# A masked maximum per head in one VectorE instruction, with the planner's slots regrouped

## The chip, the cores and the metric

One core of a Trainium2 chip runs the whole program. The metric is the device time of one execution in microseconds, from inputs in DRAM to the output in DRAM. Three runs of the kernel before took 1297.30, 1300.51 and 1302.75 us; the median is 1300.51 us.

## The reference, cut to what matters

The input is 16 sequences (batches) of 256 tokens with 256 features, in float32. Each batch goes through one block in hyperbolic space (a norm with scale and shift from a condition, full attention with 16 heads of 16 features, Möbius addition, a feed-forward part), then through a second attention with a local and a remote part, a modulated linear layer, and a feed-forward layer with four low-rank experts of which two are chosen. The change is about the scores of the second attention. Its local part lets a token see the 64 tokens that end with itself:

```python
i = jnp.arange(W)[:, None]
j = jnp.arange(2 * W)[None, :]
base = (j > i) & (j <= i + W)
...
sc = jnp.einsum('bhnid,bhnjd->bhnij', Qb, Kw) / np.sqrt(D).astype(np.float32)
sc = jnp.where(mask[None, None], sc, -jnp.inf)
p = jax.nn.softmax(sc, axis=-1)
```

The softmax subtracts, for each token and head, the greatest score among the tokens that the mask lets through. That maximum is what the changed lines compute.

## The kernel before, in words

**The batches.** `front(b)` records the first block of batch b, `back(b)` the second attention and the experts. All 16 batches are recorded, one after the other; nothing runs at that point.

**The planner.** `Plan` keeps one node per instruction (several products of TensorE that belong together are one node, a `unit`). At the end `emit` (L214) orders them. `schedule` (L254) simulates the five queues: PE (TensorE), DVE (VectorE), ACT (ScalarE), POOL (GpSimd) and SP, which issues the DMAs. `cost` (L182) gives each operation a time, `lag` the delay until another engine may use its result. Each node has a due time: its batch's number times a period, less the longest chain behind it. Of the nodes that can start first on their engine, the one due first is taken. `emit` tries 32 settings (hurry, period, limit of narrow banks), keeps the one whose simulated end is earliest, and writes the queues out in that order. Work of several batches is thus interleaved in every queue, and the order is fixed before the program starts.

**Memory.** PSUM has eight banks of 512 float32 columns. A product takes a bank when it starts and the bank is free after its last reader; `four` takes four banks for one stage. In SBUF, `spare` tiles come from three common pools: 6 slots of 1 KB per partition (t1), 18 of 2 KB (t2) and 8 of 4 KB (t4). `w_tile` gives a tile a ring of its own: pqk and qk2 with one slot of 8 KB each, p1o and p2o with one of 2 KB, xr with two of 2 KB, and xpT, gkm and gkT with one small slot each. A ring's next tile waits for all users of the one that had its slot. Small statistics (`s_tile`, L624) have rings of two, x has a ring of four.

**The local maximum.** For each batch there are four stages: two groups of features c, and two blocks of 128 query tokens qt. The first block sees 128 key tokens, the second 192. A stage fills four banks, one per quarter j of the 128 rows; in a bank lie the scores of two heads side by side, 256 or 384 columns. First four products of `ident_bf` and `maskq` (bfloat16, 128 rows deep) write the mask into the banks: 0 where a token is seen, -1e30 elsewhere (L1046). Then four score products, 32 rows deep and run beside each other in the array, add to them (L1048). Last, VectorE reduces each bank to two maxima with one `tensor_reduce` (L1054). The remote part has a stage of its own in the same manner, with `maskrq` (L1062, L1065, L1071). The 24 maxima of a token are transposed (L1077), go through DRAM (mT_dram, L1079) and come back as a row of the query tiles (L1083), so that the later score products (L1103 remote, L1166 local) give scores with the maximum taken off.

**Other lines that the prediction uses.** L784 is `project`, a product of a transposed tile with weights. L840 is the first projection to q, k and v, L974 the projection to the second q and k, L1211 the modulated linear layer, L939 the feed-forward part in the first block. L699 is the transposing of a tile through TensorE. L733 is the scale and shift behind the norm. L745 is a product of two tiles on VectorE whose sum goes to an accumulator. L872 scales q, k and v of the heads, L920 divides the first attention's result by its sum. L1289 and L1298 are the experts' low-rank and wide products; the low-rank rows come back through DRAM (low_dram). L372 is `load`, which issues the DMAs of weights.

Of the kernel before, what the change touches and what calls it, by code (L numbers as in the profile page):

```python
# [44 lines left out]
N_T1, N_T2, N_T4 = 6, 18, 8  # L45
# [20 lines left out]
class Plan:  # L66
# [5 lines left out]
    PERIODS = 65.0, 70.0, 75.0, 80.0  # L72
    HURRIES = 5.0, 6.0, 7.0, 8.0
    early = ("pqk", "qk2")
    NARROWS = 3, 4

    def __init__(self, tc):
        nc = tc.nc
        self.tc, self.nodes, self.batch, self.hold = tc, [], 0, None
        self.seen, self.slots, self.ring, self.kept, self.wide = {}, {}, {}, set(), set()  # L80
        self.phys, self.place = {}, {}
        self.real = {"pe": nc.tensor, "dve": nc.vector, "act": nc.scalar, "pool": nc.gpsimd, "sp": nc.sync}
# [46 lines left out]
    def region(self, ap, write=False):  # L129
        name, dims = ap.name if isinstance(ap, View) else ap.tensor.name, list(ap.ap)  # L130
        if ap.space == DRAM and write:
            return name, 0, P, ap.offset, ap.offset + 1
        if ap.space in (PSUM, DRAM):
            return name, 0, P, 0, 1 << 30
        step = dims[0][0]
        p0, f0 = divmod(ap.offset, step)
        return name, p0, p0 + dims[0][1], f0, f0 + 1 + sum((n - 1) * st for st, n in dims[1:])

    def note(self, eng, op, args, kw):
# [7 lines left out]
        first = self.region(outs[0])[0]  # L147
# [4 lines left out]
        if not joins:  # L152
            n = dict(
                eng=eng, ops=[], cost=0.0, batch=self.batch, pre=set(), post=set(), tiles=set(),
                id=len(self.nodes), hold=self.hold, first=first, table=None, modes=[],
# [4 lines left out]
        n["cost"] += self.cost(eng, op, outs, rest, n)  # L160
        for write, aps in ((False, rest), (True, outs)):
            for ap in aps:
                if is_ap(ap):
                    self.access(n, write, *self.region(ap, write))
# [17 lines left out]
    def cost(eng, op, outs, rest, n):  # L182

        cols = max(int(np.prod(v.shape[1:])) for v in outs + [r for r in rest if hasattr(r, "tensor")])
        if eng == "sp":
            run = min((v.ap[-1][1] if v.ap[-1][0] == 1 else 1 for v in outs + rest if hasattr(v, "tensor")), default=1)
            return 0.1 + int(np.prod(outs[0].shape)) * 4 / (2e5 if run >= 128 else 0.7e5 if run >= 32 else 0.05e5)
        if eng == "pe":
# [8 lines left out]
            if n["hold"] is not None and (lhs.shape[0] < 64 or outs[0].shape[0] < 64):  # L197
                return (0.024 if lhs.shape[0] < 64 else 0.016) + 0.00042 * cols
# [7 lines left out]
        if eng == "pool":  # L206
            if op == "affine_select":
                return 0.2 + 0.00098 * cols
            return 0.76 if ALU.pow in rest else 0.27 + (0.0021 if op == "tensor_tensor" else 0.0009) * cols
        extra = 0.06 * (op == "scalar_tensor_tensor") + 0.05 * (op == "tensor_reduce") + 0.06 * (len(outs) > 1)  # L210
        return max(0.11, 0.05 + 0.0011 * cols + extra)


    def emit(self):  # L214
# [5 lines left out]
        for tag, names in self.ring.items():  # L220
            bufs = self.slots[names[0]][1]
            for old, new in zip(names, names[bufs:]):
                behind = [m["id"] for m in users[old]]
                for u in users[new]:
                    if tag in self.early and u["eng"] != "pe":
                        for m in [nodes[m] for m in u["pre"]]:
                            if m["eng"] == "pe" and m["batch"] == u["batch"]:
                                m["pre"].update(behind)
# [5 lines left out]
        lag = lambda n: {"pe": 0.27, "sp": 2.2, "dve": 0.18, "act": 0.18}.get(n["eng"], 0.05)  # L234
# [10 lines left out]
        settings = itertools.product(self.HURRIES, self.PERIODS, self.NARROWS)  # L245
        best = min(settings, key=lambda s: self.schedule(order, users, lag, *s)[0])
        _, out, self.place = self.schedule(order, users, lag, *best)
# [6 lines left out]
    def schedule(self, order, users, lag, hurry, period, most):  # L254
# [16 lines left out]
        held, narrow = set(), 0  # L271
# [4 lines left out]
        table, mode, out = None, None, []  # L276

        def start(n):
# [5 lines left out]
            for tag, names in need.items():  # L284
                if len(pools[tag]) < len(names):
                    return None, need
                if tag == "bank" and names[0] not in self.wide and narrow + len(names) > most:
# [4 lines left out]
        while len(out) < len(nodes):  # L292
            best = None
            for e, ns in avail.items():
                cand = [(max(t, free[e]), n, need) for n in ns for t, need in [start(n)] if t is not None]
# [26 lines left out]
            n["t"], n["end"] = t, end  # L322
            out.append(n)
# [1041 lines left out]
```

## Time and profile before

| | us |
|---|---|
| median of three runs | 1300.51 |
| profiled execution, device time | 1302.17 |
| its span, first to last instruction | 1300.4 |
| PE busy (share of the span) | 1207.1 (93%) |
| DVE busy | 877.3 (67%) |
| ACT busy | 688.2 (53%) |
| POOL busy | 666.2 (51%) |
| mask products L1046, busy, 256 of them | 46.5 |
| local score products L1048, busy, 512 records | 52.5 |
| local maxima L1054, busy, 256 of them | 119.9 |

The profile comes from one execution. A float32 product leaves two records in it, a bfloat16 product one. PE is TensorE's products and PEld its weight loads. Busy time of PE is the union of modelled spans, so a product's time in the queue is better read from one start to the next. In a row of the groups, the idle time stands behind the second bar with what ended it. The granted clock of TensorE was 0.972 of full speed on the mean.

### The profile page before, as it was taken

What the parts mean: (1) busy time and instruction counts of PE and PEld (TensorE: products, weight loads), DVE (VectorE), ACT (ScalarE), POOL (GpSimd) and SP (SyncE); (2) the same over time, 40 slices, a digit from 0 to 9 for tenths busy, and PEclk for the clock granted to TensorE, in tenths of its full rate; (3) what the DMA queues carried; (4) which work ended last, traced back from release to release, by engine and by line L of the source; (5) the groups of instructions that cost most, each with busy time, mean ns of one, the idle gap of its engine ahead of it and who ended that gap; (6) DMA issues with size and microseconds to landing.
All of it is one profiled execution on the core that took longest, in us unless ns stands there. A gap on an engine that the chain in (4) does not pass through costs nothing.

```text
span 1300.4 us, 27101 instructions
## 1 busy us (share of the span) xinstructions
PE 1207.1 (93%) x9684; PEld 797.8 (61%) x9684; DVE 877.3 (67%) x2800; ACT 688.2 (53%) x1750; POOL 666.2 (51%) x1677
## 2 busy tenths in 40 slices
PE   4987999999999999999999999999999998979776
PEld 2654565757666576657666576657656665757465
DVE  5747686876869677776869677676968765573331
ACT  1555667547473755647473755646473753724210
POOL 5167566646464564646464564656455462743210
PEclk7998999999999999999999999899999999999897
DMA  6520001010100201010100101020000100000001
GB/s 193 175 61 17 23 7 35 25 29 10 40 14 18 36 17 30 16 36 9 41 14 18 35 18 31 7 43 11 23 23 17 25 2 20 1 15 7 20 2 25
DMA packets 59462, 38.70 MB, mean 30 GB/s; under 512 B 33312, under 2 KB 53792, under 8 KB 59328
## 3 DMA queue, kind: packets, MB, share of 16 engines
q1 hardware_dynamic: 59328, 36.97, 11.6%
q8 instruction: 76, 1.25, 0.5%
q14 instruction: 58, 0.48, 0.1%
HBM read 31.60 MB, written 5.36 MB: 28 GB/s over the span
## 4 chain that ended last, share of the span: by engine, by line
PE 65%; DVE 11%; POOL 10%; ACT 6%; DMA 4%; issue 3%; SPq 0%; DVEq 0%; ACTq 0%; POOLq 0%
PE bank L784 11%; PE bank L1298 6%; PE bank L904 5%; PE bank L840 5%; PE bank L891 4%; PE bank L699 4%; PE bank L939 4%; PE bank L1048 3%; PE bank L1289 2%; PE bank L1211 2%; PE bank L1153 2%; POOL t L566 2%; PE bank L1046 2%; PE bank L974 2%; ACT t L662 2%
## 5 line engine op out<-in xcount | busy, mean ns | idle before, releaser
L566 POOL TENSOR_SCALAR_AFFINE_SELECT t<-t 128x512 f32<-128x512 f32 (+2 forms) x264 | 168.2, 661 | 37.7 <-ACT t L1174 36.8
L662 ACT ACTIVATE t<-t 128x256 f32<-128x256 f32 x224 | 92.8, 423 | 148.0 <-DVE t L733 53.4
L911 ACT ACTIVATE t<-bank 128x512 f32<-128x512 f32 x256 | 132.3, 615 | 38.8 <-PE bank L904 38.6
L784 PE MATMUL bank<-wot,t 128*128 128x256 f32 x512 | 129.2, 394 | 2.1 <-POOL t L1311 1.9
L1054 DVE TENSOR_REDUCE maxima<-bank 128x2 f32<-128x384 f32 (+1 forms) x256 | 119.9, 482 | 15.1 <-PE bank L1048 15.0
L1298 PE MATMUL bank<-t,wi 128*128 128x256 f32 x512 | 130.0, 389 | 0.0
L784 PEld LDWEIGHTS bank<-wot,t 128*128 128x128 f32 x512 | 93.2, 192 | 28.0 <-issue 11.8
L1174 ACT ACTIVATE t<-bank 128x320 f32<-128x320 f32 x256 | 92.9, 446 | 19.8 <-PE bank L1166 19.3
L1298 PEld LDWEIGHTS bank<-t,wi 128*128 128x128 f32 x512 | 91.5, 192 | 18.2 <-issue 9.0
L840 PE MATMUL bank<-wqkv,t 128*128 128x512 f32 (+1 forms) x256 | 94.8, 504 | 1.4 <-ACT t L708 1.4
L699 PE MATMUL bank<-ident,t 128*128 128x128 f32 x384 | 61.4, 284 | 18.0 <-DVE t L733 11.7
L904 PE MATMUL bank<-t,t 32*128 32x512 f32 x512 | 75.7, 646 | 0.1
L1311 POOL TENSOR_TENSOR t<-t,t 128x512 f32<-128x512 f32 x32 | 43.3, 1368 | 53.4 <-DVE t L1308 52.3
L891 PE MATMUL bank<-t,vpad 128*32 128x256 f32 x1024 | 68.3, 385 | 0.1
L699 PEld LDWEIGHTS bank<-ident,t 128*128 128x128 f32 x384 | 43.8, 142 | 39.2 <-DVE t L733 13.8
L844 DVE SCALAR_TENSOR_TENSOR pqk<-bank,m1f,bqkv 128x512 f32<-128x512 f32 (+1 forms) x64 | 38.9, 614 | 40.6 <-PE bank L840 31.2
L840 PEld LDWEIGHTS bank<-wqkv,t 128*128 128x128 f32 x256 | 45.7, 193 | 33.0 <-issue 25.2
L1166 PE MATMUL bank<-qk 32*128 32x128 f32 (+1 forms) x1024 | 58.9, 330 | 6.8 <-ACT t L1174 4.8
L1304 ACT ACTIVATE t<-bank 128x512 f32<-128x512 f32 x64 | 36.3, 593 | 53.1 <-PE bank L1298 53.1
L708 ACT COPY t<-bank 128x512 f32<-128x512 f32 x80 | 47.5, 593 | 31.6 <-PE bank L699 31.4
L1308 DVE SCALAR_TENSOR_TENSOR t<-bank,t 128x512 f32<-128x512 f32 x64 | 42.3, 681 | 29.9 <-PE bank L1289 29.7
L1166 PEld LDWEIGHTS bank<-qk 32*128 32x128 f32 x1024 | 45.4, 189 | 27.3 <-issue 12.3
(322 smaller groups left out, 2856.1 us busy)
## 6 DMA issues: line engine op xcount, KB each, us to landing
ada<-ada_dram SPq DMA_DIRECT2D x32, 256.0 KB
x<-in_x_dram SPq DMA_DIRECT2D x16, 256.0 KB
ada<-ada_dram SPq DMA_DIRECT2D x32, 128.0 KB
out_dram<-t SPq DMA_DIRECT2D x16, 256.0 KB
qk<-in_w_f_dram SPq DMA_DIRECT2D x2, 1024.0 KB
t<-low_dram SPq DMA_DIRECT2D x64, 32.0 KB
t<-rho_dram SPq DMA_DIRECT2D x16, 128.0 KB
t<-in_w_ada_dram SPq DMA_DIRECT2D x3, 512.0 KB
```

What stands on the lines that cost most here:

```text
L566: pool.affine_select(out=ap, in_=ap, pattern=pattern, compare_op=ALU.is_ge, fill=fill, base=base, channel_multiplier=cm,)
L662: act.activation(junk, src, AF.Square, accum_out=dst)
L699: pe.transpose(ps[:, c, bass.ts(t, P)], src[:, t, bass.ts(c, P)], ident)
L784: pe.matmul(ps[:, t, :], chunks[c][:, bass.ts(t, P)], weights[:, c, :], start=c == 0, stop=c == n - 1)
L840: pe.matmul(ps[:, :w], uT[:, c, bass.ts(t, P)], wqkv[:, c, a : a + w], start=c == 0, stop=c == NC - 1,)
L891: pe.matmul(avs[c][quad(j), gh, :], vpad[:, kt, head(2 * c + gh, j), :], es[j][:, gh, :], start=kt == 0 and gh == 0, stop=kt == NT - 1, sk ...
L904: pe.matmul(scs[j], kT[quad(j), c, bass.ts(kt, P)], qT[quad(j), c].rearrange("p g s -> p (g s)"), start=True, stop=True,)
L911: act.activation(es[j].rearrange("p g s -> p (g s)"), scs[j], AF.Exp)
L1054: dve.tensor_reduce(mx[:, qt, m0 : m0 + 4 * NC + 1 : 4 * NC], scs[j][:, : 2 * w].rearrange("p (g w) -> p g w", g=2), AX.X, ALU.max,)
L1166: pe.matmul(scs[j][:, a : a + w], k2T[quad(j), g % 2, g // 2, bass.ts(kt, P)], q2T[quad(j), g % 2, g // 2, kt * P : kt * P + w], start=Tru ...
L1174: act.activation(e[:, k, 0:NLOC], scs[2 * pr + k][:, :NLOC], AF.Exp)
L1298: pe.matmul(hs[j][:, f, :], wi[:, c, bass.ts(2 * j + f, P)], zT[:, c, :], start=False, stop=c == NC - 1, skip_group_check=True,)
```

## The change: what it does

The four mask products of each local stage are left out. In place of one reduction per bank there are two `tensor_tensor_reduce` instructions, one for each head: each adds the mask (float32, in SBUF) to the scores in the bank, writes the sums to a bfloat16 tile `seen` that nobody reads, and puts the greatest into its column of `mx`. The remote stage keeps its mask products.

```diff
                 with plan.unit():
-                    for j in range(4):
-                        pe.matmul(scs[j][:, : 2 * w], ident_bf, maskq[:, 2 * a : 2 * (a + w)], start=True, stop=False)
                     for j in range(4):
                         pe.matmul(
                             scs[j][:, : 2 * w], qm[quad(j), c, bass.ts(qt, P)], km[quad(j), c, :, k0 : k0 + w],
-                            start=False, stop=True,
+                            start=True, stop=True,
                         )
                 for j in range(4):
-                    m0 = 4 * c + j
-                    dve.tensor_reduce(
-                        mx[:, qt, m0 : m0 + 4 * NC + 1 : 4 * NC],
-                        scs[j][:, : 2 * w].rearrange("p (g w) -> p g w", g=2), AX.X, ALU.max,
-                    )
+                    for gh in range(2):
+                        m = 4 * (NC * gh + c) + j
+                        dve.tensor_tensor_reduce(
+                            out=seen[:, :w], in0=scs[j][:, gh * w : (gh + 1) * w], in1=maskf[:, a : a + w], scale=1.0,
+                            scalar=NEG, op0=ALU.add, op1=ALU.max, accum_out=mx[:, qt, m : m + 1],
+                        )
```

The slots are regrouped. The rings of `w_tile` are gone, and their tiles come from the common pools: pqk as two tiles pq (one per token block), qk2 as q2T and k2T. The preamble's large tiles (biases, w_f1, w_f2) take common slots too and are loaded in more pieces.

```diff
-N_T1, N_T2, N_T4 = 6, 18, 8
+N_X = 6
+N_T1, N_T2, N_T4 = 6, 20, 11
...
-    PERIODS = 65.0, 70.0, 75.0, 80.0
-    HURRIES = 5.0, 6.0, 7.0, 8.0
-    early = ("pqk", "qk2")
-    NARROWS = 3, 4
+    SETTINGS = ((7, 80, 5, 1), (8, 75, 5, 1), (6, 70, 5, 0), (10, 75, 4, 1), (3, 45, 3, 0))
...
     def s_tile(shape, tag, b):
-        return plan.tile(stat, [P] + shape, tag, f"{tag}_{b}", 2, True)
+        bufs = 6 if tag in ("m1n2", "m1f", "m2n2", "m2f", "w1") else 4 if int(np.prod(shape)) <= 32 else 3
+        return plan.tile(stat, [P] + shape, tag, f"{tag}_{b}", bufs, True)
```

The planner changes with them. A product may claim, in its own node, the SBUF tiles that its result goes to, so that it isn't started before they are free (`claim`). It can be made to wait for a tile that a later instruction of its chain reads or overwrites (`wait_for`, `wait_free`). Regions of a tile are kept apart more finely (`regions`). Costs and lags have new numbers, a fifth setting holds back batches that aren't the oldest, and a DMA has a time of issue on SP and a time of transfer behind it, with at most eight under way:

```diff
+        if eng == "pe":
+            n["tiles"].update(self.claims)
+            self.claims = []
...
-            run = min((v.ap[-1][1] if v.ap[-1][0] == 1 else 1 for v in outs + rest if hasattr(v, "tensor")), default=1)
-            return 0.1 + int(np.prod(outs[0].shape)) * 4 / (2e5 if run >= 128 else 0.7e5 if run >= 32 else 0.05e5)
+            long = all(v.ap[-1][0] == 1 and v.ap[-1][1] >= P for v in outs + rest)
+            n["move"] = int(np.prod(outs[0].shape)) * 4 / (2.2e5 if long else 1.1e5)
+            return 0.4 if long else 0.7
...
+                since = free[e] if e != "sp" or len(landed) < 8 else max(free[e], landed[-8])
...
+            if e == "sp":
+                end = moved = max(end, moved) + n["move"]
+                landed.append(end + lag(n))
```

Some instructions are split by token block, so that a tile of each block can be used by itself: the scaling of q, k and v (L872) and the division of the remote heads (L1126, L1127), for instance

```diff
         for k, (eng, dst) in enumerate(((dve, qn), (dve, kn), (dve, vpad))):
-            eng.tensor_tensor(
-                dst[:, :, :, 0:HD], pq[:, :, k],
-                fh.rearrange("p (t k) h -> p t k h", k=3)[:, :, k].unsqueeze(3).to_broadcast([P, NT, H, HD]),
-                ALU.mult,
-            )
+            for t in range(NT):
+                eng.tensor_tensor(
+                    dst[:, t, :, 0:HD], pq[t][:, k],
+                    fh.rearrange("p (t k) h -> p t k h", k=3)[:, t, k].unsqueeze(2).to_broadcast([P, H, HD]),
+                    ALU.mult,
+                )
```

and the eight transposes that bring an attention's result of one token block back to tokens are one unit (`to_tokens`). What is computed stays the same.

## The prediction

> **What bounds the kernel now.** I read the busy shares first, then the slices, then three stretches, then the groups of the engines involved.
>
> ```profile
> PE 1207.1 (93%) x9684; PEld 797.8 (61%) x9684; DVE 877.3 (67%) x2800; ACT 688.2 (53%) x1750; POOL 666.2 (51%) x1677
> ...
> PE   4987999999999999999999999999999998979776
> ...
> PEclk7998999999999999999999999899999999999897
> ```
>
> TensorE is the engine near its limit, but not everywhere: the first four slices and the last five have holes. The stretches put numbers on that (length, then busy time of PE, PEld, DVE, ACT, POOL, the granted clock).
>
> ```profile
> 0.00:130.00 130.00, 97.58 (x528) 59.46 (x528) 82.69 (x289) 59.44 (x146) 65.82 (x183) 0.89 0.38 112
> 130.00:1100.00 970.00, 943.13 (x7796) 615.68 (x7794) 710.95 (x2261) 564.20 (x1443) 535.84 (x1365) 0.99 0.10 23
> 1100.00:1300.40 200.40, 166.42 (x1366) 122.67 (x1362) 83.68 (x251) 64.55 (x163) 64.50 (x129) 0.91 0.06 12
> ```
>
> TensorE is idle for 32.4 us at the start, 26.9 us in the 970 us of the middle (2.8%), and 34.0 us at the end. In the middle VectorE is busy 73% of the time, so TensorE sets the pace there, and a product taken out of its queue should be time taken off the end.
>
> [...] The timeline decides, since it shows starts and not modelled ends:
>
> ```profile
> 323.09 0.81 PE L1046 MATMUL bank<-maskq,ident_bf 128*128 128x384 bf16 x4
> 323.83 0.93 PE L1048 MATMUL bank<-t,t 32*128 32x384 f32 x8
> 324.58 1.04 PE L1289 MATMUL bank<-t,wb 32*128 32x256 f32 x16
> ...
> 339.29 0.60 PE L1046 MATMUL bank<-maskq,ident_bf 128*128 128x256 bf16 x4
> 339.82 0.71 PE L1048 MATMUL bank<-t,t 32*128 32x256 f32 x8
> 340.46 1.13 PE L1211 MATMUL bank<-t,cw 128*128 128x256 f32 x4
> ```
>
> Each group starts before the busy time of the one in front is over, and no idle time stands at any of these rows: the queue is full, and the distance from start to start is the real price.
>
> **Part 1: the mask products go.** There are 256 of them (16 batches, 4 stages, 4 banks), half 256 and half 384 columns wide. Four narrow ones take 339.82 - 339.29 = 0.53 us, four wide ones 323.83 - 323.09 = 0.74 us. The difference, 0.21 us for 4 x 128 columns, is 0.053 us per 128 columns, so the columns of four narrow ones take 0.43 us and of four wide ones 0.64 us; about 0.10 us is left in both cases. I read that as the change from 128 rows to 32 rows of the array, and it stays, since the 32-row score products still follow something 128 rows wide. So a stage loses 0.43 or 0.64 us: 32 x (0.43 + 0.64) = **34.2 us**. Upper bound: all of 32 x (0.53 + 0.74) = 40.6 us, if that 0.10 goes too. Lower bound: only the stages in the full stretch count, 970 of 1300 us, 25.5 us, because at the ends TensorE waits for others.
>
> **Part 2: VectorE's maximum.** 256 reductions, each over two heads of one bank, become 512 fused instructions of one head each (128 or 192 elements), each with an accumulator read. The nearest rows (behind the first bar the busy time in us and the mean ns of one, behind the second the idle time in front):
>
> ```profile
> L1054 DVE TENSOR_REDUCE maxima<-bank 128x2 f32<-128x384 f32 x128 | 67.8, 547 | 9.9 <-PE bank L1048 9.9
> L1054 DVE TENSOR_REDUCE maxima<-bank 128x2 f32<-128x256 f32 x128 | 52.1, 417 | 5.2 <-PE bank L1048 5.1
> ...
> L745 DVE SCALAR_TENSOR_TENSOR t<-p1o,t 128x256 f32<-128x256 f32 x32 | 12.8, 420 | 0.1
> ...
> L745 DVE DVE_READ_ACCUMULATOR t<-p1o,t 128x1 f32 x32 | 2.6, 81 | 0.0
> ```
>
> From 256 to 384 elements a reduction grows by 130 ns. L745 is the nearest to the new one: two streams and an accumulator, 420 ns for 256 elements, hence 290 ns for 128 and 355 ns for 192. By whole durations with the read behind them the pair costs 2 x (290 + 81) - 417 = 325 ns more than the narrow reduction, and 2 x (355 + 81) - 547 = 325 ns more than the wide one: 83 us over 256 pairs. That is the upper bound, since in the timeline durations on VectorE overlap: from start to start a narrow reduction takes 0.33 us and a wide one 0.46 us, L745 takes 0.346 us, and the instruction after an accumulator read starts together with it. On that scale the new ones are 0.346 - 0.13 = 0.21 and 0.28 us, and a pair costs 0.09 us more: 24 us over the run. I take 24 us, being what the queue really pays. It lies beside TensorE: VectorE in the middle goes from 73% of a batch's 73 us to some 77% of 71 us (82% by the upper bound). Without that cover it would cost 1.5 us a batch. How long four banks are held hardly changes: 0.43 to 0.64 us less in front, 4 x 0.09 = 0.37 us more behind. A cost below nothing is excluded: more instructions read the same elements.
>
> [...]
>
> **Part 3: VectorE work split per token block.** Normalised q, k and v (L872) become 96 instructions of 256 elements for 48 of 512; at 701 ns against 414 ns (L920, the same shape from a bank) that is 0.13 x 48 = 6 us. The reciprocal and product of the remote heads are halved too: 16 x (0.25 + 0.15) = 6 us. Both beside TensorE: 0.8 us a batch more. Bounds: nothing and 12 us of VectorE.
>
> **Part 4: loads and slots at the start.** Weights and bias for the preamble come in six more DMAs; an issue of L372 shows 0.42 to 0.44 us on the DMA queue of SP, so 2.6 us there. TensorE waits for a load only once (5.4 us, the first w_ada). Nothing to 2.6 us; I take nothing, because work of batch 0 covers the rest.
>
> **Part 5: the planner.** Its costs, limits and buffer rules change, and it writes out the order of every queue anew. SP's transfers are no longer summed on SP but given a landing time and a limit of eight; a product now claims, when it starts, the SBUF tile that its result goes to. What it can gain is what TensorE waits for now:
>
> ```profile
> PE bank L1103 <- DMA t<-mT_dram: 17.6, 3, 7.5
> PE bank L699 <- DVE t L733: 11.7, 3, 10.4
> PE bank L1289 <- DMA t<-low_dram: 10.7, 1, 10.7
> ```
>
> These three, 40 us, fall almost wholly at the two ends, where few batches are there to fill a gap; a better order moves them little. In the middle 27 us are spread over many short waits. Bounds: -60 us (all of the middle, half of the 66 us at the ends) and +80 us (5 us a batch, the slower rival below). I take half of the middle: **-13 us**, the ends unchanged. That is nearest to what the waits show, and it is the softest term here.
>
> **Sum**, against the profiled execution: its time 1302.2 us is the span of 1300.4 and 1.8 around it, 0.1% over the median of 1300.5. 1302.2 - 34.2 - 13 = 1255 us, with the added VectorE work hidden. What is late next in the middle is still TensorE.
>
> **Rivals.**
>
> 1. *The order gains much more.* The three long waits shrink as landing times are modelled, and deeper common buffers fill the start. For it: 66 us of idle at the ends. Against: the last batch's chain through two round trips to DRAM stays. -34 and -40 to -60: some 1222 us.
> 2. *The gain is eaten.* VectorE at 82% in bursts holds the four banks of a stage longer, and the products behind wait; the new order gains nothing. For it: 15 us of VectorE's waits at L1054 show that it works at the pace of TensorE. Against: it has a quarter of its time free. 0.325 - 0.09 us x 64 stages x 1 to 2 banks uncovered returns 15 to 30 us: 1302 - 34 + 22 = 1290 us, a range of 1283 to 1298.
> 3. *Slower: slots run out.* The rings of their own (pqk, qk2, p1o, p2o, xr and three small ones) are gone. Counted in kilobytes per partition, the 4 KB class with pqk and qk2 had room for 12 tiles and has 11; with p1o, p2o and two of xr the 2 KB class had 22 and has 20. Per batch some 16 tiles ask for the 4 KB class, and q2T and k2T are held from the projection at L974 to the last local scores. A product that claims its target waits in TensorE's queue with everything behind it. It decides when such waits exceed the gain: (34 + 13) / 16 = 2.9 us a batch over what is waited now. At 5 us a batch: 1302 - 34 + 80 - 13 = 1335 us. Against: the common pool is given by need, and the planner counts the slots when it orders.
> 4. *It does not do what it says*: the products gone but the 0.10 us change of array shape doubled. That is at most 64 x 0.10 = 6 us, inside the forecast's range.
>
> **How the numbers follow.** Forecast 1255 us (1238 to 1275), chance 0.55; rival 1, 0.20; rival 2, 0.14; rival 3, 0.11. Rival 2's upper edge is partly within 0.5% of 1300.5 us (about what a measurement of this kernel can tell from no change), so 0.05 of its chance goes there. Faster 0.84, same 0.05, slower 0.11. The range leaves out rival 3 and the far half of rival 1: 1218 to 1290 us.
>
> **What would show it.** Right: no bf16 products against the mask in TensorE's groups apart from the remote ones (L1062, L1099), busy time of PE down by 30 to 45 us, the score products at the same distance from start to start, 512 fused instructions with mean durations near 290 and 355 ns, VectorE's busy time up by 20 to 95 us, and a batch in the middle at 70 to 71 us. Wrong: fused instructions above 500 ns, idle time of PE in the middle above 60 us with waits on banks at L1048 or on tiles at L974, or a start and an end longer than 130 and 200 us.

## The result and the profile after

The changed kernel takes **1363.53 us** (median of four runs, 1359.61 to 1366.12), the kernel before 1301.45 us beside it: a ratio of **1.048 [1.0445, 1.0516]**. It is slower; the forecast was 1255 us. The profiled execution took 1366.12 us, its span is 1364.4 us.

The page of the changed kernel, with the rows that answer to those of before, and the first line of the chain that ended last:

```profile
PE 1229.7 (90%) x9418; PEld 820.1 (60%) x9428; DVE 932.0 (68%) x3646; ACT 678.6 (50%) x1742; POOL 652.1 (48%) x1677
...
PE   5999888988989998998999899998999998899776
...
PEclk8999878988999899999999998999999899899797
...
PE 48%; DVE 20%; POOL 13%; DMA 9%; issue 5%; ACT 4%; SPq 1%; DVEq 0%; POOLq 0%; ACTq 0%
```

The middle, a row of nines before, now has eights all along. In the chain VectorE holds 20% and transfers 9%. Before, VectorE held 11% and transfers 4%:

```profile
PE 65%; DVE 11%; POOL 10%; ACT 6%; DMA 4%; issue 3%; SPq 0%; DVEq 0%; ACTq 0%; POOLq 0%
```

TensorE's busy time rose by 22.6 us although 256 products are gone, since products that wait for their banks overlap less, and part of the waiting so counts as busy: the 512 records of the local scores last 501 ns on the mean, 480 before, but cover 76.1 us and not 52.5, and a narrow group takes 1.37 us from its start to that of the next group (median), 0.64 before. The granted clock fell from 0.972 to 0.939. The three stretches:

```profile
0.00:130.00 130.00, 115.17 (x660) 68.33 (x660) 98.55 (x362) 69.55 (x172) 72.48 (x203) 0.96 0.42 122
130.00:1100.00 970.00, 891.89 (x7077) 589.45 (x7086) 696.87 (x2741) 516.50 (x1340) 490.46 (x1277) 0.95 0.08 21
1100.00:1364.40 264.40, 222.66 (x1699) 162.28 (x1689) 136.59 (x544) 92.53 (x231) 89.14 (x198) 0.91 0.05 11
```

TensorE is idle for 970 - 891.89 = 78.1 us in the middle, where it was 26.9. Measured at the start of the linear layer of each batch, the way to batch 2 grew from 335.3 to 357.3 us, batches 2 to 12 from 73.95 to 77.02 us each, and the way from batch 12 to the end from 225.6 to 236.8 us: 22 + 31 + 11 us, the whole difference of the spans. What TensorE waits for, in all, times, longest:

```profile
PE bank L1153 <- DMA t<-mT_dram: 26.5, 9, 4.8
PE bank L1219 <- DMA t<-mT_dram: 14.4, 3, 6.0
PE bank L1347 <- DMA t<-low_dram: 13.2, 2, 12.0
PE bank L1094 <- DVE maxima L1101: 10.2, 17, 1.7
...
PE bank L945 <- DVE maxima L1101: 6.3, 6, 1.5
```

There are two kinds, and in the middle both are new or nearly so: transfers of the rows of maxima (mT_dram; before, three such waits of 17.6 us in all, 13.7 of them at the end), and banks that the local maximum has not left (before, 0.6 us in all). L1094 is the local score product (L1048 before), L945 the scores of the first attention, L1153 and L1219 the products that use the rows of maxima.

The clock goes with these waits. By the clock records of this trace TensorE's clock is either full or half. In the middle it is half for 106 us, in 18 pieces of 3.4 to 20.5 us; before, it was half for 10 us there. The longest piece begins at 158.1 us, among waits for banks:

```profile
160.98 1.23 PE L1094 MATMUL bank<-t,t 32*128 32x256 f32 x6 [1.69 <-DVE maxima L1101]
162.80 2.77 PE L1094 MATMUL bank<-t,t 32*128 32x256 f32 x8 [0.59 <-DVE maxima L1101]
```

```profile
158.20:178.50 20.30, 15.86 (x88) 8.28 (x88) 16.34 (x77) 8.24 (x22) 9.36 (x23) 0.50 0.04 11
```

At half clock the records of 256-column float32 products start 427 ns apart, at full clock 216. Summed over the products that took about twice their usual time, that is an estimate of 28 us in the whole run of the changed kernel, and of 12 us before. What decides when the clock is halved, no run here shows; that it is halved less where waits are taken away, e6 and e13 do (54 and 20 us of the middle for 106).

The new instructions, by form:

```profile
L1101 DVE CUSTOM_DVE_ANT_0 seen<-bank,maskf 128x192 bf16<-128x192 f32 x256 | 91.4, 357 | 27.1 <-PE bank L1094 8.5 <-DVE maxima L1101 0.3
L1101 DVE CUSTOM_DVE_ANT_0 seen<-bank,maskf 128x128 bf16<-128x128 f32 x256 | 74.4, 290 | 18.8 <-DVE maxima L1101 0.5
...
L1101 DVE DVE_READ_ACCUMULATOR2_ANT maxima<- 128x1 f32 x512 | 42.4, 83 | 0.0
```

Their durations are what was forecast (290 and 355 ns). But 46 us of idle time stand in front of them, and only 9 us of that are put down to products. The timeline shows where the rest is:

```profile
510.62 0.35 DVE L1101 CUSTOM_DVE_ANT_0 seen<-bank,maskf 128x192 bf16<-128x192 f32 x1
510.90 0.08 DVE L1101 DVE_READ_ACCUMULATOR2_ANT maxima<- 128x1 f32 x1
511.01 0.36 DVE L1101 CUSTOM_DVE_ANT_0 seen<-bank,maskf 128x192 bf16<-128x192 f32 x1
511.29 0.08 DVE L1101 DVE_READ_ACCUMULATOR2_ANT maxima<- 128x1 f32 x1
511.52 0.36 DVE L1101 CUSTOM_DVE_ANT_0 seen<-bank,maskf 128x192 bf16<-128x192 f32 x1
...
513.74 0.36 DVE L1101 CUSTOM_DVE_ANT_0 seen<-bank,maskf 128x192 bf16<-128x192 f32 x1
514.03 0.08 DVE L1101 DVE_READ_ACCUMULATOR2_ANT maxima<- 128x1 f32 x1
514.03 0.48 DVE L1272 TENSOR_SCALAR t<-bank,demod 128x256 f32<-128x256 f32 x1
```

From start to start it is 0.39 us to the second head of a bank (510.62 to 511.01) and 0.51 us to the next bank (511.01 to 511.52), not 0.28. An instruction of another line, L1272, starts together with the accumulator read at 514.03; a fused one starts 0.11 or 0.23 us after it. All 512 fused instructions write the same tile `seen`, which nobody reads, and the program makes each wait, by a semaphore of VectorE itself, until the one in front has written it.

### The profile page after: what moved, and what is told of

It is laid out like the page before. It is cut to its first block, busy times and chain, and to the rows that moved or that the text cites. A ratio compares the mean times of both kernels' runs of the same rounds, so it can differ in the third digit from the quotient of the medians.

```text
span 1364.4 us, 27678 instructions
## 1 busy us (share of the span) xinstructions
PE 1229.7 (90%) x9418; PEld 820.1 (60%) x9428; DVE 932.0 (68%) x3646; ACT 678.6 (50%) x1742; POOL 652.1 (48%) x1677
## 2 busy tenths in 40 slices
DMA packets 59630, 38.74 MB, mean 28 GB/s; under 512 B 33408, under 2 KB 53888, under 8 KB 59488
## 3 DMA queue, kind: packets, MB, share of 16 engines
q1 hardware_dynamic: 59488, 36.98, 10.5%
## 4 chain that ended last, share of the span: by engine, by line
PE 48%; DVE 20%; POOL 13%; DMA 9%; issue 5%; ACT 4%; SPq 1%; DVEq 0%; POOLq 0%; ACTq 0%
DVE seen L1101 8%; PE bank L816 7%; PE bank L1356 6%; DMA t<-mT_dram 6%; POOL t L604 4%; PE bank L877 3%; PE bank L731 3%; PE bank L945 3%; PE bank L1018 3%; PE bank L930 3%; PE bank L1094 2%; PE bank L1347 2%; PE bank L1219 2%; PE bank L1204 2%; PE bank L984 1%
## 5 line engine op out<-in xcount | busy, mean ns | idle before, releaser
L1101 DVE CUSTOM_DVE_ANT_0 seen<-bank,maskf 128x128 bf16<-128x128 f32 (+1 forms) x512 | 165.7, 324 | 45.9 <-PE bank L1094 8.5
L604 POOL TENSOR_SCALAR_AFFINE_SELECT t<-t 128x512 f32<-128x512 f32 (+1 forms) x260 | 164.2, 653 | 67.0 <-ACT t L1227 64.9
L945 PE MATMUL bank<-t,t 32*128 32x512 f32 x512 | 92.3, 726 | 8.3 <-DVE maxima L1101 6.3
L731 PE MATMUL bank<-ident,t 128*128 128x128 f32 x512 | 85.7, 289 | 8.5 <-POOL t L1250 2.9
L1094 PE MATMUL bank<-t,t 32*128 32x256 f32 (+1 forms) x512 | 76.1, 501 | 11.0 <-DVE maxima L1101 10.2
L731 PEld LDWEIGHTS bank<-ident,t 128*128 128x128 f32 x512 | 62.1, 147 | 35.2 <-POOL t L1250 6.7
L1219 PE MATMUL bank<-t,t 32*128 32x192 f32 (+1 forms) x1024 | 64.9, 355 | 20.0 <-DMA t<-mT_dram 14.4
L1219 PEld LDWEIGHTS bank<-t,t 32*128 32x128 f32 x1024 | 49.6, 207 | 45.0 <-issue 23.5
L930 PE MATMUL bank<-t,vpad 128*32 128x256 f32 x1024 | 75.8, 417 | 0.0
L930 PEld LDWEIGHTS bank<-t,vpad 128*32 128x32 f32 x1024 | 28.6, 116 | 58.3 <-issue 29.3
```

The source lines that it names most:

```text
L604: pool.affine_select(out=ap, in_=ap, pattern=pattern, compare_op=ALU.is_ge, fill=fill, base=base, channel_multiplier=cm,)
L731: pe.transpose(ps[:, c, bass.ts(t, P)], src[:, t, bass.ts(c, P)], ident)
L930: pe.matmul(avs[c][quad(j), gh, :], vpad[:, kt, head(2 * c + gh, j), :], es[j][:, gh, :], start=kt == 0 and gh == 0, stop=kt == NT - 1, sk ...
L945: pe.matmul(scs[j], kT[quad(j), c, bass.ts(kt, P)], qT[quad(j), c].rearrange("p g s -> p (g s)"), start=True, stop=True,)
L1094: pe.matmul(scs[j][:, : 2 * w], qm[quad(j), c, bass.ts(qt, P)], km[quad(j), c, :, k0 : k0 + w], start=True, stop=True,)
L1101: dve.tensor_tensor_reduce(out=seen[:, :w], in0=scs[j][:, gh * w : (gh + 1) * w], in1=maskf[:, a : a + w], scale=1.0, scalar=NEG, op0=ALU. ...
```

## The experiments

**Theory A**: the fused maximum is dear because each waits for the one in front through `seen`. Rival B: it is dear by its length and number. **Theory C**: the planner's new order loses because the write of rho (L1334 of the changed kernel, 1 KB as 256 pieces of 4 bytes) stands in front of the rows of maxima; it became C' and E below. Rival D: the new order or its slots lose by themselves. Times are medians; "setting" is the one that the planner picks from its list by its own simulation. A small edit can make it pick another, and then every queue has another order, so the text says of each experiment how its order stands.

| run | slots and order | local maximum | write of rho | us | ratio to before |
|---|---|---|---|---|---|
| before | old | reduction, mask products | 4-byte pieces | 1301 | 1 |
| changed | new | fused, one tile | 4-byte | 1363.5 | 1.048 [1.0445, 1.0516] |
| e1_seen4 | new | fused, four tiles | 4-byte | 1325.5 | 1.0158 [1.0142, 1.0174] |
| e6_seen8 | new | fused, eight tiles | 4-byte | 1301.9 | 0.9989 [0.9968, 1.0011] |
| e3_oldplan_fused | old | fused, one tile | 4-byte | 1349.4 | 1.034 [1.0309, 1.0371] |
| e14_oldplan_seen8 | old | fused, eight tiles | 4-byte | 1295.9 | 0.994 [0.9915, 0.9966] |
| e5_oldplan_unmasked | old | reduction, no mask | 4-byte | 1271.1 | 0.9745 [0.9719, 0.977] |
| e2_newplan_oldmax | new | reduction, mask products | 4-byte | 1322.4 | 1.0143 [1.0126, 1.016] |
| e7_oldmax_rho_act | new | reduction, mask products | 4-byte, ScalarE's queue | 1326.4 | 1.0178 [1.0148, 1.0209] |
| e8_oldplan_rho_act | old | reduction, no mask | 4-byte, ScalarE's queue | 1274.8 | 0.9794 [0.9762, 0.9826] |
| e9_newplan_rho_act | new | reduction, no mask | 4-byte, ScalarE's queue | 1307.9 | 1.0035 [1.0011, 1.0059] |
| e10_oldmax_rhoT | new, other setting | reduction, mask products | 128-byte pieces | 1247.2 | 0.9572 [0.9549, 0.9595] |
| e17_oldmax_rhoT_pin | new | reduction, mask products | 128-byte | 1280.7 | 0.9831 [0.9792, 0.9869] |
| e12_oldplan_unmasked_rhoT | old, other setting | reduction, no mask | 128-byte | 1283.6 | 0.986 [0.9832, 0.9888] |
| e15_before_rhoT | old | reduction, mask products | 128-byte | 1280.8 | 0.9845 [0.9828, 0.9862] |
| e16_after_rhoT | new | fused, one tile | 128-byte | 1292.9 | 0.9936 [0.9917, 0.9955] |
| e13_seen8_rhoT | new | fused, eight tiles | 128-byte | **1222.2** | **0.9381 [0.9354, 0.9407]** |
| e18_seen8_rhoT_both | new | fused, eight tiles | 128-byte, and 4-byte to a row nobody reads | 1304.7 | 1.003 [1.0016, 1.0043] |
| e11_newplan_unmasked_rhoT | new | reduction, no mask | 128-byte | 1239.5 | 0.9513 [0.9488, 0.9537] |
| e19_seen8_rhoT_set | new, other setting | fused, eight tiles | 128-byte | 1247.5 | 0.958 [0.9556, 0.9604] |

"No mask" takes the maximum over all the columns, the unseen ones too. "New" without more is the setting of the changed kernel, (7, 80, 5, 1), but for e9 (6, 70, 5, 0).

### The wait through the unread tile

e1_seen4 writes one of four tiles, by bank; the two heads of a bank still share one. The order of every queue is that of the changed kernel.

```diff
-    seen = const_tile([P, W1], "seen", BF16)
+    seen = [const_tile([P, W1], f"seen{k}", BF16) for k in range(4)]
...
-                            out=seen[:, :w], ...
+                            out=seen[m % 4][:, :w], ...
```

> The changed kernel with four tiles in turn in place of the one that the fused instructions write their sums to; the order of every queue is that of the changed kernel. Theory A (each fused instruction waits until the one in front has written the same tile): the start-to-start distance at the maximum falls from 0.40 and 0.51 us (192 elements) to 0.28 us and from 0.33 and 0.44 us (128) to 0.22 us, some 75 us of VectorE's time go, TensorE's waits on the maxima shrink, and the time falls from 1363 us to between 1270 and 1320 us. Theory B (the new order and the regrouped slots are what costs): the distance may fall, but the time stays above 1345 us.

1325.5 us, 38 us less and 5 us above A's range: the wait at the change of bank went, the 0.12 us between the two heads stayed. e6_seen8 takes the rest away, in the same order (`seen[2 * j + gh]`, eight tiles):

> The changed kernel with eight tiles in turn for the sums of the fused instructions, one per bank and head (with four tiles in turn the two instructions of a bank still wrote the same tile). The order of every queue is that of the changed kernel. Theory A: no fused instruction waits for the one in front, 0.28 and 0.22 us from start to start, another 26 us of VectorE's time go, and the time falls by 10 to 25 us below the run with four tiles (1325 us), to 1300 to 1315 us. If something other than that tile makes them wait (the maxima's tile), the distance stays at 0.40 and 0.33 us and so does the time.

1301.9 us: 62 us less than the changed kernel, by nothing but the number of tiles. Summed over the trace from each product's start to the next one's, TensorE spends 24 us less at the local scores (L1094) and 13 us less at the first attention's scores (L945), the two lines whose banks the maximum held; the rest is spread over many lines. The clock is at half for 54 us of the middle in place of 106, and the estimate of what that costs falls from 28 to 16 us. What it still waits for is mT_dram (51 us at L1153 and L1219). e3_oldplan_fused puts the fused maximum and the missing products alone into the kernel before:

> The kernel before with only the local maximum changed: no mask products, two fused instructions per bank that write one tile. Planner, slots and splits as before. Theory A: the products' 34 us are lost again to VectorE's waits, 1290 to 1340 us. Theory B: 1262 to 1275 us, the 34 us as a gain.

1349.4 us, above both ranges, so the loss does not need the new order. (The planner's setting is (7, 65, 3) here and (7, 75, 4) in the kernel before, so this is a third order.) e14_oldplan_seen8 is e3 with eight tiles, in e3's order to the row:

> The old slots and planner with the fused maximum and no mask products (e3, 1349 us), each fused instruction writing one of eight tiles in turn; the order of every engine's instructions is that of e3. Theory A (the fused instruction is dear because each waits until the one in front has written the same tile): the wait goes as it did under the new plan, where it was worth 62 us: 1282 to 1295, so some 15 us above the plain reduction over the same products (1271). Rival B (under the old plan the fused maximum is dear by its own length and by its number, two for a bank instead of one): 1325 or more.

1295.9 us: 53 us less, near A's range and far below B's. Theory A stands under both orders. The timeline of VectorE in e13_seen8_rhoT (eight tiles) shows what the same instruction takes when nothing holds it:

```profile
466.22 0.35 DVE L1102 CUSTOM_DVE_ANT_0 seen<-bank,maskf 128x192 bf16<-128x192 f32 x1
466.49 0.08 DVE L1102 DVE_READ_ACCUMULATOR2_ANT maxima<- 128x1 f32 x1
466.49 0.35 DVE L1102 CUSTOM_DVE_ANT_0 seen<-bank,maskf 128x192 bf16<-128x192 f32 x1
466.77 0.08 DVE L1102 DVE_READ_ACCUMULATOR2_ANT maxima<- 128x1 f32 x1
466.77 0.35 DVE L1102 CUSTOM_DVE_ANT_0 seen<-bank,maskf 128x192 bf16<-128x192 f32 x1
```

0.28 us from start to start, whether the bank changes or not; the next instruction starts together with the accumulator read (466.49, 466.77), which costs no slot here. A wide stage of eight is through in 2.22 us (465.94 to 468.16) and not 3.41 (510.62 to 514.03).

### The products alone

e5_oldplan_unmasked leaves the mask products out of the kernel before and keeps its reductions, which now see the unseen columns too.

```diff
-                    for j in range(4):
-                        pe.matmul(scs[j][:, : 2 * w], ident_bf, maskq[:, 2 * a : 2 * (a + w)], start=True, stop=False)
...
-                            start=False, stop=True,
+                            start=True, stop=True,
```

> The kernel before without the mask products and with its reduction unchanged, so that the maximum is taken over unseen tokens too (the softmax is the same for any such shift). This measures what the products alone are worth. Both theories: 1301 - 34 = 1267 us, with 1275 as the upper end if only the full stretch gains; VectorE as before.

1271.1 us, 33 us less than the kernel before beside it. The planner picked another of its settings for it, (7, 80, 3), so part of this may be order.

### The new order, and the write of rho

e2_newplan_oldmax keeps all that the change does to slots, claims and planner, and puts the old maximum and its mask products back.

> The changed planner, slots and splits, but the local maximum as before: four mask products and one reduction per bank. Theory A: 1275 to 1310 us, about the time of the kernel before. Theory B: 1340 us or more.

1322.4 us, between the two ranges, and a loss of 19 us where 13 were to be won. TensorE waits 29.7 us for mT_dram at the remote products. SP's queue of e2 at one batch (start, length of the issue, what is issued):

```profile
419.23 0.42 SPq L1340 DMA_DIRECT2D rho_dram<-rtx  x1
419.70 1.09 SPq L1137 DMA_DIRECT2D t<-mT_dram  x2
420.91 2.61 SPq L1335 DMA_DIRECT2D t<-low_dram  x4
428.27 0.34 SPq L1342 DMA_DIRECT2D t<-rho_dram  x1
428.65 0.56 SPq L1137 DMA_DIRECT2D t<-mT_dram  x1
```

The write of rho takes some 9 us to land. The two rows issued right behind it land at 428.4 to 428.6, with it; SP then waits for the landing (until 428.27) before it reads rho, and the last row stands behind that. In the kernel before, at the batch looked at, the rows of the batch were issued ahead of the write and landed in 1.7 to 2.4 us. Theory C blamed SP's queue, so e7_oldmax_rho_act gives the write to ScalarE's queue, TensorE's order being e2's to the row:

```diff
-        sp.dma_start(out=rho_row.rearrange("(t p) -> p t", p=P), in_=ex[:, :, E])
+        act.dma_start(out=rho_row.rearrange("(t p) -> p t", p=P), in_=ex[:, :, E])
```

> The changed planner and slots with the maximum as before (1322 us), and the write of rho to DRAM issued by ScalarE's queue in place of SP's; the order of all else is the same. Theory C (the new order puts this write, which takes about 9 us to land, in front of the rows of maxima, which then land as late): the rows land in about 2 us, TensorE's waits on mT_dram fall from 31 to under 15 us, and the time falls to 1295 to 1312 us. Rival D (the new order is worse for other reasons, such as short slots): the time stays within 5 us of 1322 us.

1326.4 us: no gain, and 25 of 96 rows still land after more than 5 us, as in e2. Theory C as stated fell. The same edit in the old order without products (e8) and in the new one (e9):

> The kernel before without the mask products, its reduction unchanged (over unseen tokens too), with the write of rho issued by ScalarE's queue. Theory C: few rows wait behind that write in the old order, so little is won in the middle; at the end, where TensorE waits 8 to 9 us on mT_dram and 10 us on low_dram, some 10 to 15 us: 1255 to 1266 us, against 1271 with SP's queue. Rival D: 1271 us.

> The changed planner and slots, no mask products, one reduction per bank over unseen tokens too, and the write of rho issued by ScalarE's queue. Theory C: what the changed planner loses is that write, so about as fast as the same with the old planner, 1255 to 1280 us. Rival D: 1285 us or more.

1274.8 and 1307.9 us: in e5's order, to the row, nothing is won by it, and the new order, with a setting of its own, is 33 us slower here too.

So the write itself was changed. In e10_oldmax_rhoT rho is copied to a padded tile, turned by one 32x32 transpose of VectorE, and written in 8 pieces of 128 bytes:

```diff
-        sp.dma_start(out=rho_row.rearrange("(t p) -> p t", p=P), in_=ex[:, :, E])
+        dve.tensor_copy(rhos[b % 2][:, 0:NT], ex[:, :, E])
+        rhoT = s_tile([PADH], "rhoT", b)
+        dve.transpose(rhoT, rhos[b % 2])
+        for t in range(NT):
+            plan.awaited = [rhoT]
+            sp.dma_start(
+                out=rho_row[t * P : (t + 1) * P].rearrange("(a s) -> a s", s=PADH), in_=rhoT[t : P : PADH, :]
+            )
```

> The kernel with the new slots and planner and the old maximum (e2, 1322 us), with rho written in 8 pieces of 128 bytes (turned by a 32x32 transpose on VectorE) instead of 256 pieces of 4 bytes. Theory C' (the small pieces land in some 9 us, and what is queued around them lands as late, SP's read of rho among it, with the last row of maxima behind that): rho's write lands in about 2 us, rows landing after more than 5 us go from 25 of 96 back to 12 or fewer, TensorE's waits for mT_dram in the middle fall from some 30 us to below 12, time 1295 to 1312. Theory D (the loss of the new slots and planner lies in banks and tiles held, or in the order itself; the slow write is met by other work anyway): 1317 to 1327, mT waits hardly less.

1247.2 us, 75 less than e2 and more than any theory gave, but the planner had picked another setting, (10, 75, 4, 1). e17_oldmax_rhoT_pin holds it to e2's, which gives TensorE e2's order to the row:

> The new slots and planner with the old maximum (e2, 1322 us), rho written in 8 pieces of 128 bytes, the planner held to e2's setting; TensorE's order is that of e2 to the row (e10 had another setting and order). Theory C': the write was worth 70 to 90 us there, as from e6 to e13, 1235 to 1255, so the new order alone is a gain of 50 us on the kernel before once the write is out of its way. If e10's 1247 came mostly from its other setting: 1270 to 1310.

1280.7 us. So 42 us are the write, and 33 us go with the setting, that is, with another order of every queue. The same two lines in e6 (e13, TensorE's order equal but for 8 of 3628 rows), in the changed kernel (e16, likewise) and in the kernel before (e15, setting held, equal to the row):

> The changed kernel with eight tiles for the unused sums (e6, 1302 us) and rho written in 8 pieces of 128 bytes. Theory C': the waits for mT_dram (51 us at two lines in e6) fall to below 20, time 1270 to 1292. Theory D: 1297 to 1305.

> The changed kernel, one tile for the unused sums, with rho written in 8 pieces of 128 bytes; TensorE's order is that of the changed kernel but for 8 of 3628 rows. If the two causes add up (80 us for the write, as from e6 to e13): 1278 to 1290. If TensorE then waits for VectorE in the place of the rows: 1300 to 1340.

> The kernel before, with rho written in 8 pieces of 128 bytes instead of 256 of 4, its planner held to the setting that it chose before; TensorE's order is the same to the row. Theory C' (the new order of SP's queue puts the slow write where the rows of maxima wait behind it, the old one does not): little is to be had here, 1285 to 1303. Rival G (the slow write costs the old order as much as the new): 1220 to 1250, and then the planner's new order is no loss of its own and no gain either.

1222.2, 1292.9 and 1280.8 us: 80, 70 and 20 us less. The 4-byte write cost each of these orders something, and the changed one three to four times as much as the old one. In the old order almost all of the gain lies behind batch 12, whose way to the end fell from 225.6 to 202.0 us. All three lie outside the ranges named for them: e13's gain is two and a half times the greatest expected, e16 is 3 us above its first range, and e15 lies between C' and G. The middle row of e13's stretches, and one wait:

```profile
130.00:1100.00 970.00, 940.99 (x7902) 636.77 (x7911) 743.91 (x3098) 569.20 (x1475) 543.95 (x1402) 0.99 0.08 22
```

```profile
PE bank L1154 <- DMA t<-mT_dram: 1.8, 2, 1.3
```

TensorE's idle time in the middle is back to 29 us, its clock to 0.99 (at half for 20 us of the middle), a batch takes 69.5 us. e13 is the fastest of all the versions run, 6.2% below the kernel before.

What in the write does it? e18_seen8_rhoT_both keeps e13's quick write and issues the slow one as well, to a row that nobody waits for:

> e13 (1222 us) with the slow write of 256 pieces of 4 bytes put back in front of the quick one, to a row that nothing reads; TensorE's order is that of e13 to the row. Theory E (the small pieces hold the transfers that are queued with them, whoever waits for them): rows of maxima land after more than 5 us again, TensorE waits 30 us or more for mT_dram, 1270 to 1305. Theory F (what hurt was SP's wait for the slow write to land, ahead of the read of rho and of all that SP issues after it): nothing waits for this write, the time stays at 1220 to 1232.

1304.7 us, all of the gain lost, at TensorE's order to the row. Its waits:

```profile
PE bank L1154 <- DMA t<-mT_dram: 42.5, 11, 6.0
PE bank L1357 <- DMA t<-low_dram: 11.7, 2, 11.2
```

Theory E stands: the small pieces hold the transfers issued beside them, whoever waits for them (24 of 96 rows land after more than 5 us, none in e13). F, SP's wait for the landing, isn't needed. The clock is at half for 61 us of the middle again. The size of a piece and the number of pieces changed together in all these runs, so which of the two does it isn't shown. From issue to the last update of the semaphore in each trace:

| | 4-byte write, median us | rows of mT_dram over 5 us, of 96 | turns of low_dram over 5 us, of 64 |
|---|---|---|---|
| before | 8.9 | 12 | 31 |
| changed | 8.5 | 33 | 48 |
| e2 | 9.1 | 25 | 26 |
| e18 | 8.3 | 24 | 42 |
| e13, e15, e16, e17 | none; 128-byte pieces 1.6 | 0 | 0 |

### Is the rest the fused instruction or the order?

e12_oldplan_unmasked_rhoT is e5 with the 128-byte write, e11_newplan_unmasked_rhoT is e13 with a plain reduction over all the columns, e19_seen8_rhoT_set is e13 held to e10's setting.

> The old slots and planner, mask products left out and the maximum taken over all the columns, the unseen ones too (e5, 1271 us), with rho written in 8 pieces of 128 bytes. Theory C': in the old order the write stands behind the rows, so little is to be had: 1262 to 1270. Theory D: 1268 to 1275, no difference. Both: the rows of maxima land as before.

> New slots and planner, rho in pieces of 128 bytes, no mask products, and in the place of the fused maximum the plain reduction over all the columns, the unseen ones too: half as many VectorE instructions at L1099, about 24 us less of VectorE's time than in e13 (1222 us); the planner takes the setting of e13, its order differs. If VectorE is beside the path once nothing waits: within 15 us of 1222. If the fused instruction still costs time at the banks: 1190 to 1207.

> e13 (1222 us) with the planner held to the setting (10, 75, 4, 1), the one that e10 had when it was 33 us faster than e17. If that gain belongs to the setting: 1185 to 1200. If it belongs to e10's own costs (each order is a throw): 1210 to 1250.

1283.6, 1239.5 and 1247.5 us. e12 is above both its ranges and 13 us slower than e5, although all its rows land in time: it had another setting, (8, 80, 4) for (7, 80, 3). e19's setting was worth 33 us in e10 and costs 25 us here, so that e10 and e19, which differ in the local maximum and its mask products alone, take the same time. e11 lies 2.5 us above its ranges, with fewer VectorE instructions than e13 and 17 us slower, in another order. So a setting moves the time by some 30 us either way, by no rule seen here, and whether the fused maximum is better or worse than a plain reduction of the same scores stays open.

## Why the prediction was wrong

Two steps failed. Part 2 put the added VectorE work at 24 us and all of it beside TensorE, at nothing in the sum, and left out a wait that cost 62 us. Part 5 put the new order at -13 us; it cost 19.

**Part 1 held, as far as the price in TensorE's queue goes.** The 32-row score products keep their price from start to start. In e13:

```profile
607.43 0.93 PE L1095 MATMUL bank<-t,t 32*128 32x384 f32 x8
608.28 1.99 PE L817 MATMUL bank<-wot,t 128*128 128x256 f32 x8
610.21 0.71 PE L1095 MATMUL bank<-t,t 32*128 32x256 f32 x8
610.85 1.13 PE L817 MATMUL bank<-wot,t 128*128 128x256 f32 x4
```

0.85 and 0.64 us; the medians over the middle are 0.86 and 0.64 in the kernel before and in e13. The 0.10 us was read rightly as the change of shape: in both, a record of a 128-row product of 256 columns starts 0.216 us before the next 128-row one and 0.309 before a 32-row one, so the change takes 0.09 us, stays, and does not double. e5 gave 33 us against 34.2, in another order.

**Part 2 failed, and this is the larger error.** "From start to start" was read off L745, whose successor writes another tile. The step gave 0.21 and 0.28 us; with eight tiles it is just that. With one tile it is 0.33 and 0.40 to the second head and 0.44 and 0.51 us to the next bank: 256 x 0.12 + 192 x 0.23 = some 75 us of waiting that no duration shows. The diff had it all: one `seen`, 512 writers, and `plan.unread` hides the tile from the planner only. Nor was it hidden beside TensorE. VectorE's busy share in the middle hardly moved, yet from the first instruction of a stage's maximum to the end of its last the median went from 1.73 to 2.95 us (narrow) and from 3.11 to 3.48 us (wide, where the kernel before had other instructions in between). With eight tiles it is 1.76 and 2.30 us. TensorE's next scores stand in the queue for these banks: "how long four banks are held hardly changes" is the sentence that broke. This is rival 2's mechanism, priced there by durations at 15 to 30 us; it was 62 (e6), and 71 with the larger pieces (e16 to e13). Neither had the clock: of the 62 us, 28 - 16 = 12 are its part by the estimate above.

**Part 5 had the wrong sign.** -13 us was forecast, +19 measured (e2). Reading the waits for mT_dram as something that falls "almost wholly at the two ends" was right for before, and did not ask what the order kept apart: the slow write of rho and most of the rows (12 of 96 landed late before, 33 in the changed kernel). With the write mended, the new order and the old one are equal (e17 1280.7, e15 1280.8 us) at these settings. The choice of a setting alone moves 33 us (e10, e17), a term that the step did not have, though its bounds held it.

Of the signs named for a right forecast, the durations came; TensorE's busy time rose by 22.6 us where it was to fall by 30 to 45, and a batch in the middle took 77 us, not 70 to 71. Of those for a wrong one, the idle time in the middle (78 us, bound 60) and waits for banks came; fused instructions above 500 ns did not, since the wait stands between them and not in them.

**Parts 3 and 4** show no loss: e17, which has both, equals e15. Their orders differ, though, so a loss of some 30 us or less could be hidden. Part 3 read 701 ns for all 48 scalings at L872, but a third of them (vpad) took 791, so its first sum is 5 us and not 6. **Rival 3** did not come: TensorE waits at L1018 (L974 before) for 0.7 us, as before.

**The sum.** The forecast missed by 109 us. The unread tile accounts for 62 (e6) and the new order for 13 + 19 = 32 (e2); 15 us are not assigned. From the changed kernel, eight tiles take off 62 us, the larger pieces 70, both 141; of the 70, the kernel before had 20 as well. From e15 to e13, the change without its two traps is worth 58.6 us, where 47 were forecast. That it comes so near is luck of the order in part. With the planner's setting held, the new maximum without its waits and without mask products is worth 58.5 us at (7, 80, 5, 1), from e17 to e13, and nothing at (10, 75, 4, 1), from e10 (1247.2) to e19 (1247.5). So the two waits, neither of which is in the sum, made the loss; how much gain the change holds without them isn't settled.

## What to carry to other kernels

An output that nobody reads is still written, and here one tile for all of them cost 62 us (e6): give consecutive instructions tiles in turn, and before pricing one from start to start look at what its successor writes. When an order of DMAs is rewritten, look for a transfer of tiny pieces and ask which rows are now issued beside it: in the four traces of the table that have the 4-byte write, 12 to 33 of 96 rows took more than 5 us to land, in the four without it none, and moving the write to ScalarE's queue left their number at 25 (e2, e7). And where a planner picks its order from a list by simulation, hold the setting before reading small differences: here it moved the time by up to 33 us. When a wait of TensorE is priced, look at the clock of the stretch behind it as well: in the changed kernel it was 0.50 for the 20.3 us from 158.2 us.

## What the runs showed of the hardware

A wait of one VectorE instruction for the write of the one in front cost 0.12 us, and 0.23 us where the bank changed too, each beyond the moment at which another instruction would have started. Taking these waits away at an unchanged order was worth 62 us (e6).

A write of 1 KB as 256 pieces of 4 bytes took 8.3 to 9.1 us to land (medians of 16 writes), and neighbours of 128-byte pieces landed as late (two rows of e2 with it, at 428.4 to 428.6); two writes of half as much in four pieces of 128 bytes take 1.6 us each. The shares on the page do not give this away. The packet lines of the changed kernel and of e13 differ by just those pieces:

```profile
q1 hardware_dynamic: 59488, 36.98, 10.5%
```

```profile
q1 hardware_dynamic: 55392, 36.97, 11.2%
```

They differ by 59488 - 55392 = 4096 packets. By the records, 4224 packets of 4 bytes went and 128 of 128 bytes came. The shares of the 16 engines' spans come to 143 and 137 us, which tells nothing of 16 writes of 9 us, and a 4-byte packet has 9 ns in its record. The records also show that these packets leave early: behind the issue of the write 256 packets of 4 bytes start within some 0.2 us, the last of them 1.1 us after the issue (medians, in each of the four traces of the table that have the write). The other 7 to 8 us, up to the landing, come behind that. What they go into isn't in the records, and stays open.
